# First batch of a graph-transformer kernel: which engine adds the mask in the units whose weights TensorE sums

## The chip, the core and the metric

The kernel runs on one core of a Trainium2 chip. The metric is device microseconds from start to end of one execution; the median of several executions counts. One execution was also recorded by the hardware profiler; durations of single instructions come from that one.

## What is computed

Sixteen graphs (batches) of 1024 nodes with 256 features go through two layers, each of them added to its input. Layer 0 is a transformer block with 8 heads of 32 features, whose attention sees only the edges of the graph; layer 1 is a graph attention with one head. Cut to what matters here:

```python
# layer 0, after a layer norm and a relu; qkv: 8 heads of 32 features, the same for q, k and v
scores = jnp.einsum('bhqd,bhkd->bhqk', qkv, qkv) * scale
mask = adj_matrix[:, None, :, :] > 0
masked = jnp.where(mask, scores, -jnp.inf)
attn = jax.nn.softmax(masked, axis=-1)
out = jnp.einsum('bhqk,bhkd->bhqd', attn, qkv)
...
mlp = jax.nn.gelu(y @ W1 + b1, approximate=False) @ W2 + b2
# layer 1
e = jax.nn.leaky_relu(logits, negative_slope=ALPHA)
e = jnp.where(adj > 0, e, NEG_INF)
attention = jax.nn.softmax(e, axis=-1)
h_prime = jnp.matmul(attention, feat)
```

## The kernel before, in words

`fast_path` does the whole work; a second path for inputs with unusual bounds is entered only by a flag and isn't run here.

**Units of attention.** The attention of layer 0 is cut into units `(qh, g, kt)`: a half `qh` of the 1024 queries (512), a group `g` of four heads, and a tile `kt` of 128 keys. A batch has 2 x 2 x 8 = 32 units, and the eight `kt` of one `(qh, g)` are called a group below; the first batch's four groups run one after the other. Function `scores` makes one unit, with keys on the partitions: four heads, 512 queries each, in two PSUM tiles of two banks (`sc[0]` for the first two heads, the first half, `sc[1]` for the other two). Each tile has one buffer only (pool `psc`, `bufs=1`), so the next unit's matmuls on a half can't start before that half was read. L995 holds the score matmuls: 32 rows by 64 columns of the array at a time, eight of them in a unit (the profile counts 16).

**Mask.** The adjacency is turned into an 8-bit float mask, 0 or -57344, on VectorE (L594), and transposed by DMA (L904). It enters the scores in one of two ways. VectorE adds it (L1015), reading PSUM and writing SBUF; then ScalarE takes the exponential in SBUF (L1018). Or TensorE adds it: `matmul` (L573, called in `scores`) multiplies the mask by an identity in 8-bit floats into the PSUM tile, before the score matmuls accumulate on top, and ScalarE takes the exponential directly out of PSUM. A masked half takes two heads, each in four quarters of 32 columns: 8 matmuls. The number `by_pe` says how many heads of the unit TensorE masks; only the first half (two heads) is ever masked so, and only in the first batch.

**Sums.** The softmax's denominator needs the weights summed over the keys. In most units the weights are added by a DMA that accumulates (`add_up`, L1054, issued on GpSimd's queue). In the first batch, units with `kt` in `SUMMED_BY_PE = (2, 4, 6, 7)` are summed by TensorE instead: `weigh` multiplies the weights by ones (`add_to_den`, L930). Their weights lie in a tile pair named `ep`; those of the other units are named `e`, or `acc` for `kt` 0. `weigh` also multiplies the weights by the values (L1031) into one PSUM bank. It is emitted one unit late: TensorE's order is scores of unit n, weighing (and the denominator) of unit n-1, scores of unit n+1.

**Order of the work.** The program is written out in the order of issue. Several generators (`stream_a` for attention, `stream_b` for the rest of a batch, `stream_c` for the norms and transposes of the next, `stream_m` for its masks, `stream_s` for weights) yield places between 0 and 16 batches, and the lowest place goes next. Beside them small steps are put off by `defer`, until a running estimate `clock[0]`, which `scores`, `weigh` and others advance, has passed their due time. An order between neighbours on each engine is then fixed. In the first batch there is no `rest` of a batch before to fill TensorE; from the second on, the feed-forward and the second layer of the batch before (`ph`, `po`, `lg`, `pa` on L573) are put between the units.

In `scores`, the exponential of the first half is emitted first, then the work of the unit before (`go_on`), then the exponential of the second half; both of VectorE's additions come before. Other work that shares the queues in the first batch: statistics and normalization of the next batch (L742 to L751 on VectorE, L804 on ScalarE, L817 and L818 on GpSimd), mask conversion (L594), which waits for fetches of the adjacency (L586), transposes of keys (L825, copied by ScalarE on L828), copies of the denominators (L942), and the products of the weight matrices.

Of the kernel before, what the change touches and what calls it, by code (L numbers as in the profile page):

```python
# [494 lines left out]
def fast_path(  # L495
# [63 lines left out]
    def ps_tile(shape, name, dtype=F32):  # L559
        return psm.tile(shape, dtype, tag="ps", name=name)  # L560

    SUMMED_BY_PE = (2, 4, 6, 7)
# [5 lines left out]
    def matmul(out, lhsT, rhs, start=True, stop=True):  # L568
        if not quarters[0]:
            nc.tensor.matmul(out, lhsT, rhs, start=start, stop=stop)  # L570
            return
        for c in range(0, P, HD):
            nc.tensor.matmul(out[c : c + HD], lhsT[:, c : c + HD], rhs, start=start, stop=stop)  # L573
# [186 lines left out]
    def defer(us, f):  # L760
        deferred.append((clock[0] + us, len(deferred), f))

        return clock[0] + us
# [151 lines left out]
    def make_turns():  # L915
        room = 3 - len(dens_open) - open_sums[0] - bool(summed or totalled) if open_sums[0] else 100
        while turns and turns[0][0] <= room:
            n, f = turns.pop(0)
            room -= n
            f()  # L920
# [7 lines left out]
    def add_to_den(den, es, start, stop):  # L928
        for j in range(GH):
            nc.tensor.matmul(  # L930
                den[j * HD : (j + 1) * HD, :], ones, es[j // 2][:, j % 2, :], start=start, stop=stop
            )
# [41 lines left out]
    def attention(b, st):  # L974
        va, kT = st["va"], st["kT"]

        def scores(qh, g, kt):
            qs = slice(qh * QW, (qh + 1) * QW)  # L980
            sc = [
                psc.tile([P, 2, QW], F32, tag=f"sc{i}", name=f"s_{b}_{g}_{qh}_{kt}_{i}") for i in range(2)
            ]

            by_pe = 2 if b == 0 and kt not in SUMMED_BY_PE else 0
            if by_pe:
                for j in range(by_pe):
                    matmul(
                        sc[j // 2][:, j % 2, :], ident8, st[qh][:, kt // 2, :, kt % 2], start=True, stop=False
                    )  # L990
                clock[0] += 0.45
            for j in range(GH):
                r = slice(j * HD, (j + 1) * HD)
                for c in range(0, P, P // 2):
                    nc.tensor.matmul(  # L995
                        sc[j // 2][c : c + P // 2, j % 2, :],
                        kT[r, g, kt * P + c : kt * P + c + P // 2],
                        kT[r, g, qs],
                        start=j >= by_pe,
                        stop=True,  # L1000
                    )
            mb = st[qh][:, kt // 2, :, kt % 2].unsqueeze(1).to_broadcast([P, 2, QW])
            es = []
            if b == 0 and kt in SUMMED_BY_PE:
                pair = midp.tile([P, 2, 2, QW], F32, tag="mid", name=f"ep_{g}_{qh}_{kt}")
            for i in range(2):
                if b == 0 and kt in SUMMED_BY_PE:
                    e = pair[:, i]
                elif kt == 0:
                    e = accp.tile([P, 2, QW], F32, tag=f"acc{i}", name=f"acc_{b}_{g}_{qh}_{i}")  # L1010
                else:
                    e = ep.tile([P, 2, QW], F32, tag="e", name=f"e_{b}_{g}_{qh}_{kt}_{i}")
                masked = sc[i]
                if 2 * i >= by_pe:
                    nc.vector.tensor_tensor(e, masked, mb, op=ALU.add)  # L1015
                    masked = e
                es.append(e)
                weights = lambda e=e, masked=masked: nc.scalar.activation(e, masked, AF.Exp, scale=SCALE)  # L1018
                if i == 0:
                    weights()  # L1020
            return es, weights

        acc = {}


        def weigh(qh, g, kt, es):
            if kt == 0:
                acc[g, qh] = pso.tile([P, QW], F32, tag="o", name=f"o_{b}_{g}_{qh}")
            o = acc[g, qh]
            for j in range(GH):  # L1030
                nc.tensor.matmul(  # L1031
                    o[j * HD : (j + 1) * HD, :],
                    va[:, kt, (g * GH + j) * HD : (g * GH + j + 1) * HD],
                    es[j // 2][:, j % 2, :],
                    start=(kt == 0),
                    stop=(kt == NT - 1),
                )
            if b == 0 and kt in SUMMED_BY_PE:
                if kt == SUMMED_BY_PE[0]:
                    dens_open[b, qh, g] = ps_tile([P, QW], f"den_{b}_{g}_{qh}")  # L1040
                add_to_den(dens_open[b, qh, g], es, kt == SUMMED_BY_PE[0], False)
                clock[0] += 0.85
            if kt == NT - 1:
                c = tmpp.tile([P, QW], F32, tag="w2", bufs=3, name=f"os_{b}_{g}_{qh}")
                nc.vector.tensor_copy(c, o)
                weighed.append((b, qh, g, c, sums[g, qh]))

        sums = {}


        def add_up(qh, g, kt, e, i):
            if b == 0 and kt in SUMMED_BY_PE:
                return
            nc.gpsimd.dma_start(sums[g, qh][i], e, accum_op=ALU.add)  # L1054

        units = [(qh, g, kt) for qh in range(NQH) for g in range(NG) for kt in range(NT)]
        for u in units:
            make_turns()
            es, rest_of_weights = scores(*u)
            go_on()  # L1060
            rest_of_weights()
            qh, g, kt = u
            if kt == 0:
                sums[g, qh] = es
            else:
                for i in range(2):
                    defer(2.0 + 1.5 * i, lambda u=u, e=es[i], i=i: add_up(*u, e, i))
            scored.append((weigh, (*u, es)))
            yield

    def go_on():
        was_weighed, was_summed, was_totalled = weighed[:], summed[:], totalled[:]
        for l in (weighed, summed, totalled):
            l.clear()
        if scored:
            f, args = scored.pop()
            f(*args)
        summed.extend(was_weighed)
        for args in was_summed:
            total(*args)  # L1080
        for args in was_totalled:
            invert(*args)
        clock[0] += 2.0
# [484 lines left out]
```

## Time and profile before

| what | value |
|---|---|
| median of 3 runs (lowest to highest) | 3477.02 us (3476.62 to 3477.64) |
| the profiled execution | 3473.33 us |
| its span | 3471.6 us |
| first mask matmul, first feed-forward matmul (`ph`) of the first batch | 21.35 us, 145.65 us |
| mask matmuls of L573 (fp8) in the first batch | 128, 379 ns each |
| mask additions L1015 of a unit that TensorE sums | 1.22 us each |
| exponential out of PSUM, out of SBUF (L1018) | 1.02 us, 1.06 us |

A profile line gives start and length in us, the engine, the line of the kernel, the operation, `output<-inputs` by the program's names, the shapes and the count of instructions that were merged in it. In brackets stands how long the engine was idle before, and what ended that. Lengths of matmuls overlap[...]: from one start to the next is the time that a block takes. PE is TensorE, PEld its loading of weights, DVE VectorE, ACT ScalarE, POOL GpSimd, and SP issues most transfers. In the profile 8 mask matmuls are one set.

### The profile page before, as it was taken

The numbers are of one execution on the slowest core, as the hardware profiler recorded it, in microseconds if no ns is written. First come the engines' busy times: TensorE is split into PE (matmuls) and PEld (weight loads), VectorE is DVE, ScalarE is ACT, GpSimd is POOL, SyncE is SP. The second block draws the span as 40 slices with busy tenths as digits, with TensorE's granted clock in tenths as the row PEclk, the third lists the DMA queues.
The fourth block names the chain that finished last, engine by engine and source line by source line (L and its number), as shares of the span: only waits on it lengthen the run. The fifth ranks groups of instructions, "written<-read, shape, count | busy, mean of one in ns | idle before, by whom it ended". The sixth has DMA issues, their size and how long they took to land. (4 is left out here: it accounts for less than half of the span.)

```text
span 3471.6 us, 118944 instructions
## 1 busy us (share of the span) xinstructions
PE 3429.9 (99%) x52446; PEld 1652.8 (48%) x52446; DVE 2742.5 (79%) x5186; ACT 1858.7 (54%) x2184; POOL 1414.1 (41%) x1708
## 2 busy tenths in 40 slices
PE   7999999999999999999999999999999999999998
PEld 2344444444444444444444444444444444444477
DVE  6778788787887878888887887878878788887754
ACT  5655555555555555555555555555555555555522
POOL 4444443434434344443434434444343444434220
PEclk9999999999999999999999999999999999999999
DMA  8799989999899998989989899998999989899730
GB/s 199 147 178 177 188 158 191 178 189 188 163 190 178 187 192 166 182 168 194 193 162 184 169 187 189 180 187 165 191 176 190 190 162 189 171 193 182 149 64 14
DMA packets 281902, 598.56 MB, mean 172 GB/s; under 512 B 94880, under 2 KB 130080, under 8 KB 281376
## 3 DMA queue, kind: packets, MB, share of 16 engines
q0 software_dynamic: 124416, 453.04, 71.2%
q1 hardware_dynamic: 156672, 137.56, 15.8%
q8 instruction: 414, 6.78, 0.8%
q14 instruction: 112, 0.92, 0.1%
q10 hardware_dynamic: 288, 0.26, 0.0%
HBM read 104.21 MB, written 16.78 MB: 35 GB/s over the span
## 5 line engine op out<-in xcount | busy, mean ns | idle before, releaser
L1018 ACT ACTIVATE e<-e 128x1024 f32<-128x1024 f32 x852 | 896.4, 1057 | 950.0 <-DVE e L1015 713.1
L1054 POOL DMA_DIRECT2D acc<-e x864 | 756.3, 891 | 1467.2 <-DMA acc<-e 673.5
L1015 DVE TENSOR_TENSOR e<-s,mk 128x1024 f32<-128x1024 f32 x852 | 1003.7, 1217 | 191.6 <-PE s L995 148.2
L995 PE MATMUL s<-kT 32*64 32x512 f32 x8192 | 587.0, 616 | 3.3 <-DVE e L1015 1.2
L1031 PE MATMUL o<-e,va 128*32 128x512 f32 x3456 | 462.5, 605 | 1.7 <-ACT e L1018 1.7
L573 PE MATMUL pa<-gw,e 128*32 128x258 f32 x7648 | 455.5, 381 | 0.0
L573 PE MATMUL lg<-fT,uT 128*32 128x256 f32 x7680 | 448.6, 379 | 0.0
L573 PE MATMUL ph<-yT,w 128*32 128x256 f32 x7808 | 447.5, 379 | 0.0
L573 PE MATMUL po<-w,hid 128*32 128x256 f32 x7680 | 439.6, 379 | 0.0
L573 PEld LDWEIGHTS ph<-yT,w 128*32 128x32 f32 x7808 | 259.9, 110 | 197.4 <-issue 42.4
L573 PEld LDWEIGHTS po<-w,hid 128*32 128x32 f32 x7680 | 251.7, 110 | 207.4 <-issue 61.9
L573 PEld LDWEIGHTS lg<-fT,uT 128*32 128x32 f32 x7680 | 259.1, 110 | 189.4 <-issue 38.7
L573 PEld LDWEIGHTS pa<-gw,e 128*32 128x32 f32 x7648 | 251.9, 110 | 201.4 <-issue 49.6
L1290 ACT ACTIVATE e<-e,shift 128x512 f32<-128x512 f32 x256 | 183.1, 717 | 187.7 <-DVE e L1289 160.2
L1284 DVE SCALAR_TENSOR_TENSOR e<-lg,gw,mk 128x256 f32<-128x256 f32 x512 | 223.1, 477 | 71.7 <-PE lg L573 61.2
L1187 DVE TENSOR_TENSOR hid<-ph,b1c 128x512 f32<-128x512 f32 x256 | 175.5, 687 | 88.5 <-PE ph L573 76.7
L1031 PEld LDWEIGHTS o<-e,va 128*32 128x32 f32 x3456 | 68.8, 108 | 352.6 <-issue 223.2
L995 PEld LDWEIGHTS s<-kT 32*64 32x64 f32 x8192 | 123.2, 130 | 171.4 <-issue 106.2
L1289 DVE SCALAR_TENSOR_TENSOR e<-e 128x512 f32<-128x512 f32 x256 | 195.7, 765 | 8.8
L1018 ACT ACTIVATE acc<-acc 128x1024 f32<-128x1024 f32 x124 | 130.9, 1057 | 125.1 <-DVE acc L1015 121.0
L1015 DVE TENSOR_TENSOR acc<-s,mk 128x1024 f32<-128x1024 f32 x124 | 146.0, 1217 | 22.0 <-PE s L995 19.2
L817 POOL TENSOR_TENSOR nrm<-nrm,g 128x256 f32<-128x256 f32 x128 | 111.8, 874 | 61.4 <-DVE nrm L751 61.4
(144 smaller groups left out, 3805.6 us busy)
## 6 DMA issues: line engine op xcount, KB each, us to landing
acc<-e POOLq DMA_DIRECT2D x864, 512.0 KB, 6.2
adj<-in_adj_dram SPq DMA_DIRECT2D x248, 256.0 KB, 5.7
h<-in_x_dram SPq DMA_DIRECT2D x64, 256.0 KB, 6.2
xb<-in_x_dram SPq DMA_DIRECT2D x128, 128.0 KB, 4.5
out_dram<-z SPq DMA_DIRECT2D x128, 128.0 KB, 4.0
adj<-in_adj_dram SPq DMA_DIRECT2D x4, 512.0 KB, 7.0
mk<-mq SPq DMA_TRANSPOSE x128, 6.3
w<-in_L_gnn_W_dram SPq DMA_DIRECT2D x2, 1024.0 KB, 8.1
```

The lines of the kernel that those rows point to most:

```text
L573: nc.tensor.matmul(out[c : c + HD], lhsT[:, c : c + HD], rhs, start=start, stop=stop)
L817: nc.gpsimd.tensor_mul(nrm, nrm, g1)
L995: nc.tensor.matmul(sc[j // 2][c : c + P // 2, j % 2, :], kT[r, g, kt * P + c : kt * P + c + P // 2], kT[r, g, qs], start=j >= by_pe, stop= ...
L1015: nc.vector.tensor_tensor(e, masked, mb, op=ALU.add)
L1018: weights = lambda e=e, masked=masked: nc.scalar.activation(e, masked, AF.Exp, scale=SCALE)
L1031: nc.tensor.matmul(o[j * HD : (j + 1) * HD, :], va[:, kt, (g * GH + j) * HD : (g * GH + j + 1) * HD], es[j // 2][:, j % 2, :], start=(kt = ...
L1054: nc.gpsimd.dma_start(sums[g, qh][i], e, accum_op=ALU.add)
L1187: nc.vector.tensor_tensor(hid[:, f0 : f0 + 2, :], ph, b1c[:, f0 : f0 + 2].unsqueeze(2).to_broadcast([P, 2, CW]), op=ALU.add,)
L1284: nc.vector.scalar_tensor_tensor(e[:, j, :], lg[:, j, :], gw[:, kt, D : D + 1], st[c // 2][:, kt // 2, qs, kt % 2], op0=ALU.add, op1=ALU.add,)
L1289: nc.vector.scalar_tensor_tensor(e, e, ALPHA, e, op0=ALU.mult, op1=ALU.max)
L1290: ready = defer(2.5, lambda: nc.scalar.activation(e, e, AF.Exp, bias=shift))
```

## The change

In the first batch every unit now gets the mask of its first half from TensorE, also the units that TensorE sums. For `kt` 2, 4, 6 and 7 of each group, `by_pe` becomes 2: eight mask matmuls go ahead of the scores, the score matmuls of heads 0 and 1 accumulate on them (`start=j >= by_pe`), the addition of the first half on VectorE is left out (`if 2 * i >= by_pe`), and the exponential of the first half reads PSUM and writes the `ep` tile. The second half is as before. The estimate `clock[0]` grows by 0.45 in each of these units.

```diff
@@ -982,7 +982,7 @@
                 psc.tile([P, 2, QW], F32, tag=f"sc{i}", name=f"s_{b}_{g}_{qh}_{kt}_{i}") for i in range(2)
             ]
 
-            by_pe = 2 if b == 0 and kt not in SUMMED_BY_PE else 0
+            by_pe = 2 if b == 0 else 0
             if by_pe:
                 for j in range(by_pe):
                     matmul(
```

## The prediction

> **What bounds the kernel now.** I read the page's table of busy time first, then the engines' busy time by stretch, then the waits of TensorE in the one stretch that the change touches, and last the timeline of that stretch. The page says which engine the whole kernel hangs on:
>
> ```profile
> PE 3429.9 (99%) x52446; PEld 1652.8 (48%) x52446; DVE 2742.5 (79%) x5186; ACT 1858.7 (54%) x2184; POOL 1414.1 (41%) x1708
> ```
>
> TensorE (PE) is busy 99% of the span, VectorE (DVE) 79%. The chain at the end of the page is only the last 3 us and tells nothing here. The change is confined to the first batch, whose attention lies between 21.35 us (first mask matmul) and 145.65 us (first matmul of the stage that follows). By stretches (columns: stretch, its length, busy us of PE, PEld, DVE, ACT, POOL with counts, granted clock of TensorE, DMA share, GB/s):
>
> ```profile
> 29.50:145.60 116.10, 109.52 (x1244) 34.26 (x1248) 83.06 (x147) 71.60 (x88) 48.52 (x62) 0.97 0.85 171
> 145.60:345.60 200.00, 196.22 (x3040) 92.53 (x3040) 158.20 (x302) 107.97 (x124) 85.66 (x103) 1.00 0.91 173
> ```
>
> In the first batch TensorE is idle for 6.6 of 116 us, and busy time hides more: a matmul that waits for a PSUM bank in the middle of its set is drawn as busy. TensorE's own waits in that stretch (us in total, times, longest):
>
> ```profile
> PE s L573 <- DVE ep L1015: 5.3, 5, 2.3
> PE s L995 <- DVE ep L1015: 0.6, 2, 0.3
> ```
>
> Nearly all of them are the wait of the next unit's first matmul for VectorE's mask addition of a unit that TensorE sums (`ep`). These are the units that the change alters. One of them in the timeline (start, length, engine):
>
> ```profile
> 46.83 1.11 PE L995 MATMUL s<-kT 32*64 32x512 f32 x16
> 47.87 1.06 PE L1031 MATMUL o<-e,va 128*32 128x512 f32 x8
> 47.98 2.35 DVE L1015 TENSOR_TENSOR ep<-s,mk 128x1024 f32<-128x1024 f32 x2 [1.65 <-PE s L995]
> 49.24 2.19 ACT L1018 ACTIVATE ep<-ep 128x1024 f32<-128x1024 f32 x2 [1.81 <-DVE ep L1015]
> 49.26 2.22 PE L995 MATMUL s<-kT 32*64 32x512 f32 x16 [0.32 <-DVE ep L1015]
> ...
> 51.41 1.12 PE L1031 MATMUL o<-ep,va 128*32 128x512 f32 x8
> ```
>
> Both score tiles are ready 1.15 us after the scores began (46.83 to 47.98). VectorE frees them one after the other: the first 1.22 us later (TensorE goes on at 49.26, 2.43 us after the scores began), the second at 50.33, so that the next scores take 2.15 us to the next start instead of 1.04. A unit whose first half TensorE masks already looks like this:
>
> ```profile
> 57.23 0.61 PE L573 MATMUL s<-mk,ident 128*32 128x512 fp8e5 x8
> ...
> 57.78 1.11 PE L995 MATMUL s<-kT 32*64 32x512 f32 x16
> ...
> 58.82 1.07 PE L1031 MATMUL o<-acc,va 128*32 128x512 f32 x8
> 58.93 1.02 ACT L1018 ACTIVATE e<-s 128x1024 f32<-128x1024 f32 x1 [0.92 <-PE s L995]
> 59.08 1.23 DVE L1015 TENSOR_TENSOR e<-s,mk 128x1024 f32<-128x1024 f32 x1 [0.90 <-issue]
> ```
>
> ScalarE takes the first half straight from PSUM while VectorE takes the second: the two releases come side by side. The worst stall of the batch:
>
> ```profile
> 132.19 0.43 DVE L594 TENSOR_SCALAR mq<-adj 128x512 fp8e5<-128x512 int32 x1 [0.81 <-DMA adj<-in_adj_dram]
> ...
> 133.13 2.35 DVE L1015 TENSOR_TENSOR ep<-s,mk 128x1024 f32<-128x1024 f32 x2
> ...
> 134.40 1.04 PE L573 MATMUL s<-mk,ident 128*32 128x512 fp8e5 x8 [2.29 <-DVE ep L1015]
> 135.37 2.14 PE L995 MATMUL s<-kT 32*64 32x512 f32 x16
> ```
>
> VectorE was held by a mask conversion that waited for a fetch; TensorE stood still for 2.3 us behind it and then ran slow sets.
>
> [...] The trace has 0.55 us from mask to scores (57.23 to 57.78)[...]. [...] the mask set took 0.97 us to the next start instead of 0.55, with a granted clock of 0.77 and 0.81 in the two 4 us slices from 132. [...] 99% busy here contains the stretched sets counted below.
>
> **The change part by part.** It touches 4 units (kt 2, 4, 6, 7) in each of 4 groups of the first batch: 16 units. SP and GpSimd keep their instruction order, VectorE's loses 16 entries, and from the second batch on the order is the same on every engine. No DMA is added or moved.
>
> *Added on TensorE:* 16 mask sets of 8 matmuls. From mask to scores is 0.55 us. Where nothing waits, the block before gets shorter: denominator to scores takes 1.03 (45.80 to 46.83), denominator to mask 0.85 (56.38 to 57.23), so the set adds 0.85 + 0.55 - 1.03 = 0.37. Ends 16 x 0.37 = 5.9 and 16 x 0.55 = 8.7; I take the estimate's 0.43: **+6.9 us**, all on the path, since TensorE is the bound.
>
> *Removed on VectorE:* 16 additions of 1.22 us, 19.5 us of an engine that isn't the bound; in itself worth nothing. *ScalarE:* 16 exponentials read PSUM instead of SBUF, 1.02 against 1.06 us: nothing by itself.
>
> *The stalls.* I took undisturbed starts (scores 1.04 us, weighing 0.88, denominator 0.86, or 1.03 ahead of scores or transposes, transposes 0.58, mask 0.55) and added up what each TensorE block of the first batch takes beyond, from 29.55 to 145.65 us. In us, by group (g1 to g4) and by the pair of units between which it lies:
> - kt 1 to 2: g1 0.28, g3 0.48, g4 0.53
> - kt 2 to 3: g1 3.82, g2 0.28, g3 0.19, g4 1.37
> - kt 4 to 5: g1 0.97, g2 1.04, g3 0.37, g4 3.91
> - kt 5 to 6: g2 0.74
> - kt 6 to 7: g1 1.52, g2 1.58, g3 0.92, g4 0.92
>
> The sum is 6.6 + 3.6 + 2.0 + 6.7 = **18.9 us**; between kt 7 and the next group's kt 0 there is none, since two blocks cover it.
>
> *What is late next.* With the mask on TensorE, ScalarE releases the first half: 1.15 + 1.02 + about 0.06 = 2.23 us after the scores begin (90.11 to 92.34 shows just that). TensorE's cover is 1.04 + 0.88 = 1.92 where there is neither denominator nor transpose between: 0.3 left. The second half comes free 1.15 + 1.22 = 2.4 after, while the next scores start 2.23 + 0.55 = 2.8 after: no stall left. Stepping through the batch with that:
> - g1: kt 2 to 3 keeps 1.0 (VectorE gets to the addition at 32.97 as before, behind `nrm` that waits for GpSimd; the second half is free at 34.19, the weighing starts 1.07 after, as at 50.33 to 51.41), kt 4 to 5 and 6 to 7 0.3 each: 1.6
> - g2: 0.3 at kt 4; 0.5 at kt 5 to 6 (addition late, behind mask conversion and statistics); at kt 6 ScalarE has two rectifications (L804, 1.08 us) and the preceding exponential, which waited for VectorE, queued ahead: 1.3. Sum 2.1
> - g3: 0.2
> - g4: 0.2 and 0.3, and at kt 4 to 5, where the second half still waits for VectorE behind the fetch: 1.1 if that fetch lands as much earlier as everything else, 4.6 if it lands when it did. Its transfers were issued from 122.83 and it was still awaited at 132.19, with a DMA share of 1.07 in 120 to 140 us, so I take halfway: 2.85. Sum 3.3
>
> Left: 7.2 us (5.5 to 9.0). Behind ScalarE's exponential now wait the next unit's mask and scores; behind VectorE's single addition only the second exponential, the weighing and the second half of the next scores.
>
> *Sum:* -18.9 + 6.9 + 7.2 = **-4.8 us** in the first batch. After it TensorE is 98 to 100% busy and gets the same order of work, so the end moves by as much. The profiled execution took 3473.33 us (span 3471.6 and 1.7 around it); the median of the runs is 3477.02, 3.7 above, and I move that: 3477.0 - 4.8 = **3472.2 us**.
>
> **The rivals.** *B, more goes.* The fetch moves along, the residues vanish in the looser VectorE queue (only the 0.3 at six places stays, 1.8), and the masks cost 0.43: -18.9 + 6.9 + 1.8 = -10.2, so 3466.8; with 3.5 of residue 3468.5. For it: VectorE's total falls from 83 to 64 us of 116. Against it: the rectifications and fetches don't go away. *C, given back.* The stall moves to fetches and to the second half throughout (residue 11 to 12, that is, about two thirds of the stalls stay): 3476 to 3477. For it: VectorE waited 5.8 us for fetches in this stretch; against: only one of these waits sits in front of an addition that TensorE awaited for long. *D, slower.* One mechanism: the first exponential of a unit stands in ScalarE's queue behind the second one of the unit before, and that one still waits for VectorE. If the first release comes no earlier than today in all 16 units, no stall goes and the masks come on top: +6.9 to +8.7, so 3483.9 to 3485.7. It decides from the point where the stalls left exceed 18.9 - 6.9 = 12 us. Against it: before kt 2, 4 and 6 ScalarE mostly idles (26.6 us of waiting for VectorE's `ep` additions in this stretch). That the change doesn't do what it says is excluded by the instruction order.
>
> **How the numbers follow.** Chances: forecast (3469.5 to 3475.8, the bounds of masks and residue together) 0.60, B 0.19, C 0.15, D 0.06. The measurement tells apart about 0.2%, 7 us. B lies mostly beyond it and a tail of the forecast does: faster 0.22; slower only most of D: 0.05; the same 0.73. The range leaves out D, the upper edge of C and the lower one of B: 3467.5 to 3477.8.
>
> **What would show it.** The first `ph` matmul at about 140.9 instead of 145.65 us, 256 mask matmuls on L573 instead of 128, 16 fewer additions, waits of `s L573` on VectorE's `ep` gone and short ones on ScalarE's in their place, the clock at 1.00 near 132 to 140, and the same difference at the end as at 145 us. It is wrong if L573 waits for ScalarE by more than half a microsecond in most units (D), if the second half of the scores stays stretched (C), or if the shift at 145 us isn't found at the end.

## The result, and the profile after

| kernel | runs | median us (lowest to highest) |
|---|---|---|
| before | 20 | 3474.66 (3464.70 to 3487.18) |
| changed | 20 | 3474.51 (3464.04 to 3487.67) |

The ratio is 0.9999, with a 95% interval of 0.9987 to 1.0010, that is -4.5 to +3.5 us. The time lies in the range on record, and "the same" was the likeliest class. But the forecast of -4.8 us is just outside the interval, so the sum behind it has to be looked at. That the time lies in the range is no proof of the sum, since the range leaves room for no gain at all. The profiled execution of the changed kernel has a span of 3472.7 us, 1.1 longer than that of before; single executions of either kernel scatter over more than 20 us.

The page's first line of the changed kernel has the 128 added mask matmuls (and as many weight loads), 16 fewer operations on VectorE, and nothing else:

```profile
PE 3429.6 (99%) x52574; PEld 1653.4 (48%) x52574; DVE 2721.5 (78%) x5170; ACT 1858.0 (54%) x2184; POOL 1414.6 (41%) x1708
```

The first batch's stretch, then TensorE's waits between 29 and 145.6 us (columns as before):

```profile
29.50:145.60 116.10, 111.88 (x1424) 34.82 (x1416) 67.30 (x132) 73.56 (x88) 49.26 (x63) 0.99 0.85 173
```

```profile
PE ptos L966 <- issue: 1.8, 1, 1.8
PE s L573 <- ACT ep L1018: 0.8, 3, 0.5
PE s L995 <- DVE ep L1015: 0.8, 1, 0.8
```

VectorE is busy for 67.3 us instead of 83.1. The 5.3 us that `s L573` waited for VectorE's `ep` became 0.8 us of waiting for ScalarE's, as the forecast said. New is the first line: a wait at `ptos` that no semaphore explains. The pair kt 6 and 7 of the first group, in the timeline:

```profile
44.16 1.11 PE L995 MATMUL s<-kT 32*64 32x512 f32 x16
45.21 1.06 PE L1031 MATMUL o<-e,va 128*32 128x512 f32 x8
45.32 1.02 ACT L1018 ACTIVATE ep<-s 128x1024 f32<-128x1024 f32 x1 [0.86 <-PE s L995]
45.41 1.22 DVE L1015 TENSOR_TENSOR ep<-s,mk 128x1024 f32<-128x1024 f32 x1 [2.05 <-PE s L995]
46.39 0.61 PE L573 MATMUL s<-mk,ident 128*32 128x512 fp8e5 x8
...
46.94 1.11 PE L995 MATMUL s<-kT 32*64 32x512 f32 x16
47.98 1.07 PE L1031 MATMUL o<-ep,va 128*32 128x512 f32 x8
```

ScalarE and VectorE now work side by side, the mask starts 2.23 us after the scores (44.16 to 46.39), and the next scores take 1.04 us instead of 2.15. From the scores of kt 6 to those of the next group's kt 0 it is 6.81 us (44.16 to 50.97); it was 7.62 (46.83 to 54.45).

The first `ph` starts at 142.9 us; it was 145.65. Of the gain only 2.8 us is there, and this is why:

```profile
67.70 0.69 PE L573 MATMUL p_w_a<-a1c,stage 128*32 128x1 f32 x32
68.33 0.33 PE L966 MATMUL ptos<-ident,os 128*128 128x128 f32 x1
70.48 0.80 PE L966 MATMUL ptos<-ident,os 128*128 128x128 f32 x3 [1.83 <-issue]
71.21 1.04 PE L573 MATMUL s<-mk,ident 128*32 128x512 fp8e5 x8
72.18 1.94 PE L995 MATMUL s<-kT 32*64 32x512 f32 x16
```

Four transposes of one tile into one bank: the first runs, the other three wait for 1.8 us, though they have the same operands and no wait of their own. Behind it the mask set takes 0.97 us to the next start instead of 0.55, and the scores are drawn with 1.94 us instead of 1.11; the clock records show one window of 3.4 us with a granted clock of 0.50, from 70.5 us; such a window is called slow below. Before the change the same four transposes ran in one piece:

```profile
71.77 0.66 PE L966 MATMUL ptos<-ident,os 128*128 128x128 f32 x4
72.36 1.11 PE L995 MATMUL s<-kT 32*64 32x512 f32 x16
```

The trace's DMA records tell what TensorE waited for. The page's third part has a queue of kind "instruction", q8:

```profile
q8 instruction: 415, 6.80, 0.8%
```

Each of its 415 packets is 16,384 bytes, and between two of them TensorE runs 255 instructions in the mean, so I take these to be TensorE's instructions. One packet moved from 68.0 to 69.0 us, while TensorE stood still, and TensorE went on 1.5 us after it had landed. I call this a standstill below. The suspicion is that TensorE's own instructions come late; the experiments test it. Ahead of it lie the products of the weight matrices (`p_wm`, `p_w_a`), the densest stretch of the batch: between the instruction packets at 54.9 and 68.0 us, 466 instructions started.

### The profile page after: what moved, and what is told of

It is laid out like the page before. It is cut to its first block, busy times and chain, and to the rows that moved or that the text cites. A ratio compares the mean times of both kernels' runs of the same rounds, so it can differ in the third digit from the quotient of the medians.

```text
span 3472.7 us, 119190 instructions
## 1 busy us (share of the span) xinstructions
PE 3429.6 (99%) x52574; PEld 1653.4 (48%) x52574; DVE 2721.5 (78%) x5170; ACT 1858.0 (54%) x2184; POOL 1414.6 (41%) x1708
## 5 line engine op out<-in xcount | busy, mean ns | idle before, releaser
L995 PE MATMUL s<-kT 32*64 32x512 f32 x8192 | 578.3, 615 | 0.9 <-DVE ep L1015 0.8
L573 PE MATMUL pa<-gw,e 128*32 128x258 f32 x7648 | 454.6, 381 | 0.0
L573 PE MATMUL lg<-fT,uT 128*32 128x256 f32 x7680 | 449.7, 379 | 3.0 <-issue 2.9
L573 PE MATMUL ph<-yT,w 128*32 128x256 f32 x7808 | 447.0, 379 | 0.0
L573 PE MATMUL po<-w,hid 128*32 128x256 f32 x7680 | 439.7, 379 | 0.5 <-issue 0.5
L573 PEld LDWEIGHTS ph<-yT,w 128*32 128x32 f32 x7808 | 259.0, 110 | 197.9 <-issue 42.5
L573 PEld LDWEIGHTS lg<-fT,uT 128*32 128x32 f32 x7680 | 259.7, 110 | 192.5 <-issue 42.5
L573 PEld LDWEIGHTS po<-w,hid 128*32 128x32 f32 x7680 | 250.7, 110 | 209.6 <-issue 63.6
L573 PEld LDWEIGHTS pa<-gw,e 128*32 128x32 f32 x7648 | 251.4, 110 | 200.7 <-issue 49.1
```

What stands on the lines that cost most here:

```text
L995: nc.tensor.matmul(sc[j // 2][c : c + P // 2, j % 2, :], kT[r, g, kt * P + c : kt * P + c + P // 2], kT[r, g, qs], start=j >= by_pe, stop= ...
```

## The experiments

The long kernel's scatter (some 6 us) hides what a first batch can gain, so most kernels below are cut to the first two batches: `B = 2` behind `B, N, D = x.shape` in `fast_path`; the outputs of the other 14 are left out. Their line numbers are one to four higher. All ten were timed in five rounds, on three occasions and chips; the long kernel before, timed beside them each time, had medians of 3473.94, 3473.70 and 3475.84 us, which is 0.3 us in 514. One execution of each has its trace kept. Times in us:

| kernel | median (lowest to highest) | against the two-batch kernel before | first `ph` in its trace |
|---|---|---|---|
| t2_before | 514.44 (513.39 to 515.79) | | 144.3 |
| t2_after | 516.06 (511.62 to 518.58) | +1.6 | 144.0 |
| t2_release | 507.75 (506.40 to 509.52) | -6.7 | 137.3 |
| t2_masks | 521.46 (518.90 to 523.87) | +7.0 | 149.7 |
| t2_before_pad80 | 514.29 (512.23 to 516.87) | -0.2 | 145.5 |
| t2_after_pad176 | 509.97 (506.51 to 510.88) | -4.5 | 142.0 |
| t2_before_thin | 514.59 (513.68 to 515.35) | +0.2 | 142.8 |
| t2_after_thin | 512.20 (511.09 to 514.85) | -2.2 | 141.2 |
| t2_four_pad240 | 524.11 (522.94 to 525.95) | +9.7 | 156.9 |
| t2_after_p176_early | 518.34 (516.31 to 521.48) | +3.9 | 148.7 |

### The change in two batches, whole and in parts

> The kernel before, cut to its first two batches (B = 2, the other 14 outputs are left out), so that a few microseconds can be told from the scatter of 3475 us. Time about 148 + 212 + 151 = 510 us (first batch's attention, one step from batch to batch, what follows the last one, from the trace of before). The first ph matmul at 145.6 us as in the long kernel.

> The changed kernel, cut to two batches in the same way. Theory (the first batch gains what the stalls cost beyond the masks, and the gain is there at the end, but the long kernel's scatter hides it): 5 to 7 us less than the two-batch kernel before, ph starts near 140 us. Rival (the gain is given back after the first batch): ph as early, but the end within 1 us of the two-batch kernel before. Rival (there is no gain in the first batch): both within 1 us.

The expected gain isn't there: +1.6 us. The ratios to the long kernel before, 0.1481 (0.1477 to 0.1484) and 0.1482 (0.1475 to 0.1489), can't be told apart. The trace has the standstill again, at the same transposes, 2.9 us long, and four slow windows ahead of the end, where t2_before has one (mean granted clock 0.978 and 0.989 in these two executions). So the gain isn't hidden by scatter alone, and it isn't simply given back after the first batch: in this trace it is missing in the first batch already. The five executions differ, though: 511.62 us at a mean granted clock of 0.990, 512.88 at 0.985, and 516.06 to 518.58 at 0.977 to 0.980, while t2_before has 513.39 to 515.79 at 0.989 to 0.991. Whether the two quicker ones had the standstill, and the slow window behind it, isn't known.

t2_release leaves the mask of that half out of 16 units:

```diff
-            by_pe = 2 if b == 0 else 0
+            by_pe = 2 if b == 0 and kt not in SUMMED_BY_PE else 0
...
-                if 2 * i >= by_pe:
+                if 2 * i >= (2 if b == 0 else 0):
```

> Two batches; in the summed units of the first batch the mask of the first half is left out altogether (neither TensorE nor VectorE adds it, so these weights are unmasked), and ScalarE reads PSUM: the earlier release without its price. Theory: the stalls go without masks on top, 18.9 - 7.2 = 11.7 us less than the two-batch kernel before, up to 13.4; so 6 to 7 us less than the two-batch changed kernel. Rival (second halves and fetches set the pace): no better than the changed kernel.

-6.7 us, not -11.7. The earlier release alone is worth little more than half of what I had put down. But the 7.2 us left over in that sum were worked out with the mask sets in place, whose 0.55 us stand ahead of the next scores while VectorE frees the second half; so this miss concerns the sum for t2_release, not that of the prediction. What TensorE waits for in that kernel, from 29 to 140 us:

```profile
PE s L996 <- DVE e L1016: 2.0, 3, 1.0
PE s L996 <- DVE ep L1016: 1.7, 2, 1.4
PE s L996 <- ACT ep L1019: 0.8, 1, 0.8
```

With nothing in between, TensorE soon stands at the second half, which VectorE still frees.

t2_masks has both additions in the first half:

```diff
-                if 2 * i >= by_pe:
+                if 2 * i >= by_pe or (b == 0 and kt in SUMMED_BY_PE):
```

> Two batches; TensorE adds the mask in the summed units, and VectorE adds it again in the first half (the mask is then twice as large, the weights the same): the price without the earlier release. Theory: 16 sets at 0.43 us are 6.9, less some 3.3 where a set fills time in which the scores would have waited for a second half (kt 6 to 7: 4 x 0.5, kt 1 to 2 and 5 to 6: 1.3): 3.6 us more than the two-batch kernel before (2 to 6). Rival (TensorE has slack in the first batch and the sets cost nothing): within 1 us.

+7.0, not +3.6. Its trace has the standstill too:

```profile
73.44 0.33 PE L967 MATMUL ptos<-ident,os 128*128 128x128 f32 x1
75.43 0.49 PE L967 MATMUL ptos<-ident,os 128*128 128x128 f32 x3 [1.66 <-issue]
```

That unit took 9.85 us from scores to scores and 7.51 in t2_before; the next one, in the slow window from 76.6 us, took 4.12 and 3.04. Of these 3.4 us some 0.4 is the set added in the first of the two, so about 3.0 belong to the standstill and the window. Without them the first `ph` would be some 2.5 later than in t2_before (an estimate from one trace each), at the lower end of the expected 2 to 6. t2_release, which has no added instructions, has no standstill. So it comes with the added instructions, not with the earlier release.

### Where the instruction packets end

If the place matters where a packet of instructions ends, idle instructions far ahead must move it. TensorE waits for its first operands until 15.7 us, so they should cost nothing there (t2_before_pad80, with 80 of them, took 514.29 us, t2_before 514.44):

```diff
     nc.vector.tensor_copy(ident8, ident, saturate=False)
+    pad = ps_tile([P, HD], "pad")
+    for _ in range(88):
+        nc.tensor.matmul(pad[:HD], ident8[:, :HD], ident8[:, :HD], start=True, stop=True)
```

> Two batches of the changed kernel, with 88 such idle matmuls and 88 weight loads ahead: 80 + 176 = 256 instructions, about one piece, so that the piece's end lies behind the dense products as in the kernel before. Theory (instruction pieces): the standstill at ptos goes, 3 to 4.5 us less than the two-batch changed kernel, 2 to 3 us less than the two-batch kernel before, ph starts near 139.5 us. Rival (mask sets): the standstill stays, time as the two-batch changed kernel.

The same mask sets, and no standstill:

```profile
67.87 0.72 PE L574 MATMUL p_w_a<-a1c,stage 128*32 128x1 f32 x32
68.52 0.66 PE L970 MATMUL ptos<-ident,os 128*128 128x128 f32 x4
69.11 0.61 PE L574 MATMUL s<-mk,ident 128*32 128x512 fp8e5 x8
69.65 1.11 PE L999 MATMUL s<-kT 32*64 32x512 f32 x16
```

The time is 509.97: 6.1 less than t2_after, 4.5 less than t2_before (ratios to the long kernel 0.1464, 0.1458 to 0.1469, against 0.1481), and its slowest execution is faster than the fastest of either. The rival, that the mask sets themselves make TensorE stand, falls.

The counterpart puts 40 such matmuls ahead of the kernel before:

> Two batches of the kernel before, with 40 idle 32x32 mask-type matmuls and their 40 weight loads on TensorE ahead of everything, while it waits for its first operands: 80 more instructions, as many as the change puts ahead of the ptos transposes of the second group. Theory (TensorE's instructions come in 16 KB pieces of about 255; the change moves a piece's end into the dense weight products, where the next piece arrives too late): TensorE now stands still at ptos for 2 to 3 us in this kernel too, followed by a slow-clock window: 3 to 4.5 us more than the two-batch kernel before, ph starts 3 to 4 us later. Rival (the standstill comes from the mask sets themselves, or by chance): no standstill at ptos, time as the two-batch kernel before.

```profile
72.66 0.44 PE L970 MATMUL ptos<-ident,os 128*128 128x128 f32 x2
73.85 0.44 PE L970 MATMUL ptos<-ident,os 128*128 128x128 f32 x2 [0.75 <-issue]
```

The transposes are split now in this kernel too, 1.3 us after a packet landed, so the place of the packet's end is confirmed. The count confirms it further: in all five traces with a stop at these transposes (this one, the changed kernel, t2_after, t2_masks and all_batches, below) it comes after exactly 1217 recorded instructions of TensorE (matmuls and weight loads, counted from the start of the trace). But the wait is 0.75 us, no slow window follows in this trace, and the time is as before, though one of the five executions took 516.87 us at a granted clock of 0.975. This miss says that the place isn't enough: how late the packet lands differs too. In the four kernels with a full standstill it landed 0.3 (changed kernel), 1.7 (t2_after), 0.4 (t2_masks) and 0.6 us (all_batches, below) after TensorE had stopped; here it landed about 0.6 us ahead of that. The rate at which TensorE uses its instructions up tells these five traces from the rest: the last 255 instructions up to the 1217th started within 3.8 to 4.0 us, and within 6.3 to 12 us in the nine other traces. The packet itself took 2.4 us to move in t2_after and t2_masks, and 0.9 to 1.2 in the other three; why is not shown (the DMA share from 60 to 80 us was 1.02 to 1.14 in all five, and 1.13 in before). How much of each wait belongs to the rate and how much to the transfer wasn't separated.

The other way is to thin out the dense stretch. The products with one column are no longer cut into quarters:

```diff
-                    matmul(
+                    (matmul if n > 1 else nc.tensor.matmul)(
                         pp,
                         lhs[:, kc, oc * P : (oc + 1) * P],
```

> Two batches of the kernel before, in which the four products with one column (p_w_a) aren't cut into quarters: 96 fewer instructions in the dense stretch ahead of ptos, the same result. Theory (pieces): 1 us less than the two-batch kernel before for the shorter products, no standstill at ptos. Rival (quarters were cheap): within 0.5 us.

> Two batches of the changed kernel with the same uncut products. Theory (the change's gain of 5 to 6 us is real and is eaten by the standstill in the dense stretch and the slow clock behind it): the standstill is gone or under 1 us, and the time is 4 to 6 us less than the two-batch kernel before with uncut products. Rival (the gain is lost elsewhere after the first batch): within 1.5 us of it.

Neither has a standstill at `ptos`. The kernel before gains nothing (+0.2; I had expected 1 us less). The changed kernel is 2.4 us faster than its partner, less than the expected 4 to 6, and the two intervals just touch (ratios to the long kernel 0.1472 to 0.1480 and 0.1479 to 0.1484).

### The full kernel with moved packets

> The full changed kernel (16 batches) with the 176 idle instructions ahead. Theory (the standstill at ptos and the slow clock behind it ate the gain): 4 to 5 us less than the kernel before, ratio 0.9986, though a single execution scatters by some 6 us and five rounds give no more than about 3 us either way; the surer sign is in the trace: no standstill at ptos, ph starts near 140 to 142 us. Rival (the gain is lost later): ph as early, ratio 1.000 or above.

This kernel was timed in 22 runs beside 27 of before on one chip: 3468.78 us (3462.27 to 3475.89) against 3475.84 (3466.37 to 3491.44). The ratio is 0.9978, 0.9969 to 0.9988: 7.6 us faster by that ratio (4.2 to 10.8). Its interval and that of the changed kernel's ratio (0.9987 to 1.0010) only just touch; the two were measured on different occasions, so that it beats the changed kernel is likely and not shown to the same degree. The starts of each unit's scores (us, from one trace each) show where the first batch's share arises:

```
unit                      before    changed    changed, 176 ahead
group 1, kt 3              34.78      33.40      32.65
group 2, kt 3              64.88      61.83      61.82
group 2, kt 4              72.36      72.18      69.45
group 2, kt 5              75.41      75.86      72.29
group 4, kt 4             130.00     127.74     125.05
group 4, kt 6             139.32     135.85     132.41
batch 2, first unit       147.54     144.72     141.41
```

At kt 3 of the second group both changed kernels are about 3.05 us ahead of the kernel before. The standstill and the slow window behind it take 3.57 us off one of them within two units (75.86 against 72.29), and the difference between them stays between 2.7 and 3.6 us from there to the second batch (3.31 at it). At the second batch the gain is 2.8 us with the standstill and 6.1 without it.

These traces have scatter of their own. The kernel before reaches the second batch at 147.54 us here, and at 146.20 in t2_before; the two-batch kernels t2_after and t2_after_pad176 reach it at 145.79 and 143.81, so there the gain is 0.4 us with the standstill and 2.4 without it. And the execution of after_pad176 whose trace was kept is one of its fastest (3462.89 us, where the median is 3468.78). So 2.4 to 6.1 us without the standstill and 0.4 to 2.8 with it is what the traces show.

Later in these traces nearly all units take the same time to a hundredth of a microsecond (452 of the last 478 from scores to scores, between before and the changed kernel), and single events make the difference. The largest are, in the kernel before, 4.1 us about 237 to 259 us, where VectorE waited for an accumulating DMA (4.5, 0.9 and 2.0 us ahead of three additions), and 3.7 us about 1830 us, at a slow window (granted clock 0.50 for 3.4 us from 1827.15); in the changed kernel 1.4 us from a slow window at 162.7 us (again 0.50 for 3.4 us), 3.8 us about 2360 us, and 5.5 us from a second standstill:

```profile
329.32 1.48 PE L573 MATMUL lg<-fT,uT 128*32 128x256 f32 x24
333.68 1.08 PE L573 MATMUL lg<-fT,uT 128*32 128x256 f32 x8 [2.88 <-issue]
```

Again an instruction packet landed 1.4 us ahead of its end, and the granted clock was 0.50 for 3.4 us from 333.3 us. In after_pad176 no wait by "issue" is among TensorE's listed waits behind 145 us (the longest is 1.3 us, for ScalarE), so the idle instructions seem to have moved that packet as well. At the last unit's scores the traced execution of after_pad176 is 12.3 us ahead of that of before, and 6.1 of these are there at the second batch; what of the median's 7.6 us belongs to which is open.

### The price of a mask set, and two more places

all_batches masks the first half in all 16 batches (`by_pe = 2`), one round:

> The full kernel with the first half of every unit masked by TensorE in all 16 batches: 15 x 32 = 480 more sets where the page shows TensorE without waits. Theory (a set costs 0.37 to 0.55 us where it replaces no stall): 178 to 264 us more than the changed kernel, 206 at 0.43. Rival (VectorE's releases pace the later batches too): under 100 us more, or less time.

3690.99 us, 216.5 more than the changed kernel's 3474.51, for 480 sets: 0.45 us each, with 0.43 taken. The rival falls; VectorE's releases don't pace the later batches.

t2_four_pad240 masks all four heads in the first batch (`by_pe = 4`, 120 idle matmuls ahead):

> Two batches; in the first batch TensorE adds the mask of all four heads, so VectorE adds none, and ScalarE reads both halves from PSUM; 240 idle instructions ahead keep the piece's end off the dense products. Theory (the second half's release is mostly covered already): 32 sets at 0.43 us are 13.8 more, less up to 5 of stalls that still hang on VectorE: 9 to 14 us more than the two-batch changed kernel with 176 idle instructions. Rival (VectorE's additions still hold back most units): within 4 us of it.

14.1 us more than t2_after_pad176 for 32 sets, 0.44 each: just above the expected 9 to 14. Nearly nothing of the price comes back. How much still hung on VectorE's additions isn't shown by this, since new waits stand in their place: in the second group, at 69.20 us, a mask set waits 1.2 us for ScalarE.

In t2_after_p176_early the next masks are turned two units earlier (`- 0.33`, `- 0.13` for `- 0.27`, `- 0.07` in `stream_m`):

> Two batches of the changed kernel with 176 idle instructions, and the steps that fetch, convert and turn the next masks put 0.06 of a batch (two units) earlier in the order. Theory (in the last group VectorE waits for fetches between two additions, which keeps 3 to 4 us in the units before ph): these units shorten by 2 to 4 us and the end with them. Rival (the fetches are late because the transfers are busy): the wait moves to another unit, time within 1.5 us.

Both theories miss: +8.4 us against t2_after_pad176. The timeline of the second group shows where a good part of it comes from (in t2_after_pad176 the same unit, from the scores of kt 3 to those of kt 4, took 7.6 us; here it took 15.2):

```profile
67.96 0.43 DVE L746 BATCH_NORM_STATS2 st_a<-h 128x6 f32<-128x256 f32 x1 [5.94 <-DMA h<-in_x_dram]
...
71.06 0.25 DVE L960 RECIPROCAL rl<-ptds 128x16 f32<-128x16 f32 x1
71.22 0.10 DVE L803 SCALAR_TENSOR_TENSOR nm<-mv_a,rs_a 128x2 f32<-128x2 f32 x1
...
71.36 1.93 PE L574 MATMUL p_wm<-stage,stage 128*32 128x256 f32 x16 [5.14 <-DVE nm L803]
```

With the mask fetches issued earlier, the load of x came late: VectorE's statistics waited 5.9 us for it, the reciprocal and `nm` stood in its queue behind them, and TensorE waited 5.1 us for `nm`. That wait isn't in t2_after_pad176. The last group, kt 4 to kt 6, for which the edit was made, did not shorten either (6.80 and 3.45 us to the next scores, 2.83 and 4.87 in t2_after_pad176). So the transfers' wait moved and grew. More fetch buffers weren't tried.

## Why the prediction was right or wrong, step by step

**What bounds, and where the stalls are: right.** `s L573` waiting on VectorE's `ep` is gone, and short waits on ScalarE's stand in its place, at most 0.5 us (predicted 0.3, and 1.3 in one unit).

**Price of a mask set, 0.43 us: right** (0.45 in all_batches, 0.44 in t2_four_pad240). The figure was the author's estimate; the trace of before had shown only the two ends around it, 0.37 and 0.55.

**Stalls that go, 18.9 less 7.2 us: the size fits where no standstill lies in between.** From the scores of kt 2 in the first group, where the prediction began to count, to the first `ph` it is 116.1 us in the kernel before (29.55 to 145.65) and 111.1 in after_pad176 (28.51 to 139.57); in t2_before it is 116.4 and in t2_after_pad176 111.3. That is 5.0 and 5.1 us less, where the sum said 4.8. If the sets take the 6.9 us put down for them, some 7 us of stalls are left, as predicted; this is an estimate, because the runs show only what stalls and sets make together. It is rough, too: t2_after_pad176 comes to these scores 2.8 us later than t2_before, and part of that delay is made up in the next unit (3.2 us to the next scores instead of 6.6).

t2_release, without the sets, is 109.4 us long there. So the sets cost 1.9 us beside it and not 6.9, and nearly all else that they take fills waits that stay open without them. Two executions of each say the same: 506.40 and 506.41 us for t2_release at a granted clock of 0.990 and 0.991, 506.51 and 506.63 for t2_after_pad176 at 0.992. "The second half comes free 2.4 after, while the next scores start 2.8 after: no stall left" holds with the set's 0.55 us in place, and t2_release, where the next scores can start 2.23 after, doesn't test it. Single residues did move: at kt 6 of the second group, with 1.3 us put down, it took 4.0 us to the next scores in after_pad176 and 5.2 in t2_after_pad176, where 3.3 are undisturbed (83.0 to 86.3 us in after_pad176). In the fourth group the fetch wait moved from one conversion to the next: in the changed kernel kt 4 to kt 6 took 8.1 us (9.3 before), but from there to the second batch it took 8.9 (8.2 before).

**The sum of -4.8 us in the first batch: right in size for the stalls and the masks alone, within what these runs can tell** (-4.5 in two batches; -2.4 and -6.1 at the second batch of the two-batch and the long kernel; all without the standstill; -2.4 with uncut products), **and wrong for the kernel as it is.** That the time fell into the range all the same is luck: the range was wide enough for a gain that something unforeseen took away. The term that was missing is the standstill with the slow window behind it: 3.6 us within two units, and 3.3 of them at the second batch. The step that failed is the price of the addition, "**+6.9 us**, all on the path, since TensorE is the bound": it counts what the added instructions cost on the array and not that they move the ends of the instruction packets. At this place that meant 1.8 us of standstill, and 3.6 with the window behind it.

**"After it TensorE ... gets the same order of work, so the end moves by as much": right for the rhythm of the units, not for single executions.** Most unit times repeat to a hundredth of a microsecond, but standstills, slow windows and late accumulations of 1 to 6 us come on top. The prediction named as a sign of being wrong that "the shift at 145 us isn't found at the end". In the two traces it isn't: 2.8 us at the first `ph`, 0.7 at the last unit's scores, and the span is 1.1 longer.

**Rivals.** D, ScalarE's queue making it slower, didn't happen: the waits on its first exponential sum to 0.8 us. C ends where the time ended, but not by its mechanism: it had 11 to 12 us of stalls left, where some 7 fit the kernels without a standstill, and the standstill took the gain instead. The clock near 132 us did not stay full in every kernel: t2_after still had a slow window at 133.5 us, while the changed long kernel had none there (granted clock 1.00 from 120 to 140 us).

**Slips of the sum.** 16 x 0.55 is 8.8 us, not 8.7. The range up to 3477.8 doesn't leave out the upper edge of C, which ends at 3477. Nothing above hangs on either.

## What to carry to other kernels

Here an edit that put 80 more instructions on TensorE ahead of the transposes moved the end of an instruction packet into the densest stretch of the first batch. So after an edit that adds instructions, look in the changed profile for waits by "issue" inside one group of like matmuls (1.8 us here), and for a packet of the instruction queue that lands just ahead of their end (1.5 us here). The wait and the slow window behind it took 3.3 of the 6.1 us that the edit gains at the second batch without them, and idle instructions in a stretch where the engine waits anyway (until 15.7 us here) were a cheap way to test for it and to be rid of it. To measure 5 us in a kernel that scatters by 6, cut it to the part that matters, and compare unit times in the traces: here 452 of the last 478 repeat to a hundredth of a microsecond. Take more than one trace of each kernel for it, since here two traces of the kernel before reached the second batch 1.3 us apart.

## What the runs showed of the hardware that was not expected

- The instruction queue moved 415 packets of 16,384 bytes in the changed kernel, one for 255 of TensorE's instructions in the mean. TensorE stood still for 1.8, 2.9, 1.7 and 2.1 us at the same transposes in the changed kernel, t2_after, t2_masks and all_batches, each time after 1217 recorded instructions. In all of them, and in t2_before_pad80, it went on 1.2 to 1.5 us after the packet had landed.
- A stop of 1.3 us (between 154 and 175 us in the two-batch kernels) was followed by a slow window of 3.4 us in some traces (t2_after, at 164.2 us) and not in others (t2_before). At the standstills, the window came in all four kernels just named (in the changed kernel at a granted clock of 0.50, from 70.5 us).
